# Weights cut to their own widths, shorter spreads, and a planner with other numbers, in a four-layer image kernel

## The chip, the cores and the metric

The kernel runs on one core of a Trainium2 chip. A core has TensorE (matrix products; PE in the profile, PEld for its weight loads), VectorE (DVE), ScalarE (ACT), GpSimd (POOL) and SyncE (SP, which issues transfers). The metric is the device time of one execution in microseconds (us); lower is better.

## The reference

The input is four images of 96 channels and 64x64 pixels. They go through four layers; the parts that this change touches are:

```python
# layer 0: normalize, 3x3 depthwise conv + SiLU, four-direction selective scan, gate, project
delta = softplus(dts + delta_bias)
def step(h, inp):                       # along 4096 pixels, for 192 channels x 16 states x 4 directions
    h = exp(d_t[..., None] * A) * h + (d_t * u_t)[..., None] * b_t[:, :, None, :]
    return h, einsum('bkdn,bkn->bkd', h, c_t)
...
# layer 1: deformable 3x3 convolution
v00, v01, v10, v11 = gather(y0, x0), gather(y0, x0 + 1), gather(y0 + 1, x0), gather(y0 + 1, x0 + 1)
sample = (1-wy)*(1-wx)*v00 + (1-wy)*wx*v01 + wy*(1-wx)*v10 + wy*wx*v11
...
# layer 2: Fourier mixing over the pixels, then a feed-forward layer in 8-bit floats
# layer 3: linear attention, then the same kind of feed-forward layer
```

Offsets and masks of layer 1 (27 values a pixel) come from a 3x3 convolution over 96 channels. Before most layers each pixel is normalized over its channels.

## The kernel before

The program is built by a planner in Python. One chain of units is the scan: 4 images x 4 directions x 4 stretches of 1024 pixels x 3 groups x 8 = 1536 units. Each unit spreads its inflow over 128 partitions with TensorE, multiplies and scans on VectorE, weighs on GpSimd, and is folded by TensorE:

```python
    def inflow(self, u):
        u.spread = self.net.clock.add(PE, 1.1, self.scanned[1])
        db = self.ps.tile([128, 2, CH], F32, name=f"db{u.key}", tag="db", bufs=2)
        for h in range(2):
            self.net.nc.tensor.matmul(db[:, h, :], lhsT=self.rep[:96, u.s % 4, :],
                rhs=u.du[u.s // 4][:, h * CH : (h + 1) * CH], start=True, stop=True)      # L872
    def recur(self, u):
        ...
        nc.vector.tensor_mul(u.db, u.db, u.bc[:, 0, :])                                   # L885
        nc.vector.tensor_tensor_scan(u.along(u.hh), u.along(u.da), u.along(u.db), first, ALU.mult, ALU.add)  # L888
    def weigh(self, u):
        ...
        self.net.nc.gpsimd.tensor_mul(u.hh, u.hh, u.bc[:, 1, :])                          # L897
    def total(self, u, v):
        ...                                    # 8 products of 32 columns into py, L915
```

The order in which a unit's parts are emitted[...]:

```python
            for stage, m in ((self.inflow, n + 1), (self.decay, n + 1)):
                if at(m) is not None:
                    stage(at(m))
            if n % 2 == 1 and at(n - 5) is not None:
                self.total(at(n - 5), at(n - 4))
```

Between the units two streams of side work are let in: one runs the work ahead of the scan and the layers 2 and 3 of finished images, the other the end of layer 0 and layer 1. A virtual clock decides how much, from costs written at each step (`cost(pe=2.4)`), from how far an engine may be ahead, and from a pace per unit:

```python
PE, DVE, ACT, POOL = range(4)
AHEAD = (2.0, 1.5, 3.0, 4.0)
BESIDE = 6.0
PACE = 4.9
...
    def has_room(self, work, ready):
        ...
        return all(not w or e <= now + a for w, e, a in zip(work, self.ends, AHEAD))
```

When the scan is over, the rest of the side work runs alone.

Many weights are padded with zero columns to 128[...], and the rows of the result that belong to the padding are not read:

```python
    def wide(m, n=128):
        return np.concatenate([m, np.zeros((*m.shape[:-1], n - m.shape[-1]))], axis=-1).astype(f)
    ...
    a["wom"] = wide(om.transpose(1, 2, 0))      # 27 columns of offsets and masks -> 128
    a["wdc"] = wide(...)                        # 96 -> 128
    a["cen96"] = wide(np.eye(96) - 1.0 / 96)
```

The normalization: centre with a product (L457), square, sum each chunk's squares into a row of its own with a mostly zero weight (L468), take the root, and spread the row back over the partitions (L483):

```python
            pc = self.mm(f"lnc{key}_{j}")
            nc.tensor.matmul(pc, lhsT=cen, rhs=x[:, cs], start=True, stop=True)            # L457
            ...
            nc.tensor.matmul(var, lhsT=self.to_row[C][:C, 7 - j : 135 - j], rhs=sq, ...)   # L468: 128 columns, one not zero
    ...
    def spread(self, rstd, j, n, key):
        pb = self.mm(f"lnb{key}_{j}")
        row = self.ident[:, j : j + 1].to_broadcast([128, 128])
        self.nc.tensor.matmul(pb, lhsT=row, rhs=rstd, start=True, stop=True)               # L483
        return pb[:n]
```

The offset convolution of layer 1, nine products a chunk, and the step sizes of layer 0, whose weight holds seven rows that are not zero among 103:

```python
                    nc.tensor.matmul(po, lhsT=wom[:, k, :],
                        rhs=pad[:, r0 + dy : r0 + dy + NR, dx : dx + W], ...)              # L1118
    ...
            nc.tensor.matmul(o, lhsT=dtw[:, k, m], rhs=xdbl[q, j], start=True, stop=True)  # L734
```

The sampling multiplies the gathered corners by their weights and sums the four by transposes that accumulate in one bank:

```python
                        for c in range(4):
                            nc.tensor.matmul(pt[:, k, :], lhsT=g[:, k0 + k, c * C : (c + 1) * C], rhs=net.ident,
                                is_transpose=True, start=(c == 0), stop=(c == 3))          # L1241
```

Of the kernel before, what the change touches and what calls it, by code (L numbers as in the profile page):

```python
# [20 lines left out]
L = H * W  # L21
# [23 lines left out]
def prepare(x, **w):  # L45
# [4 lines left out]
    def wide(m, n=128):  # L50

        return np.concatenate([m, np.zeros((*m.shape[:-1], n - m.shape[-1]))], axis=-1).astype(f)

# [27 lines left out]
    a["w_in"] = c(np.concatenate([wi[:, :128], wi[:, 128:192], wi[:, 128:192], wi[:, 192:], np.zeros((C, 64))], axis=1).astype(f))  # L81
# [3 lines left out]
    xpp = np.zeros((2, 128, DI), f)  # L85
# [3 lines left out]
    xpp[:, 64 + R + 1 : NX] = xp[2:, R:]  # L89
# [4 lines left out]

    dtp = np.zeros((NX, KG, DI), f)
    dtp[2 * NS : 2 * NS + R + 1, :2] = dtw[:2].transpose(2, 0, 1)
    dtp[64 : 64 + R + 1, 2:] = dtw[2:].transpose(2, 0, 1)
    a["dtw"] = dtp
# [7 lines left out]
    a["wo_a"] = wide(wo[:128])  # L106
    a["wo_c"] = wide(wo[128:])
# [4 lines left out]
    a["wom"] = wide(om.transpose(1, 2, 0))  # L112
    ob = w["L1_conv_offset_b"]
    put(V_OMB, np.concatenate([ob[0::2], ob[1::2], w["L1_conv_mask_b"]]))
    a["wdc"] = wide(w["L1_conv_weight"].reshape(C, C, 9).transpose(1, 2, 0))
# [8 lines left out]
    a["w2"] = wide(w["L2_attn_w2"].T.reshape(2, 96, C).transpose(1, 0, 2))  # L124
    for n in (2, 3):
        a[f"f{n}w1"] = c(w[f"L{n}_ffn_W1"].T)
        a[f"f{n}w2"] = wide(w[f"L{n}_ffn_W2"].T.reshape(3, 128, C).transpose(1, 0, 2))
# [3 lines left out]
    a["wff"] = wide(w["L3_attn_Wff"])  # L131
# [5 lines left out]
    a["cen96"] = wide(np.eye(96) - 1.0 / 96)  # L137
    cen = (np.eye(DI) - 1.0 / DI).astype(f)
    a["cen_a"] = wide(cen[:128], 256)
    a["cen_c"] = wide(cen[128:], 256)  # L140
# [55 lines left out]
AHEAD = (2.0, 1.5, 3.0, 4.0)  # L196
# [3 lines left out]
PACE = 4.9  # L200
# [132 lines left out]
class Net:  # L333
# [3 lines left out]
    def __init__(self, ctx, tc, ins):  # L337
# [5 lines left out]
        for name in ("vecs", "ident", "cen96", "grp3"):  # L343
            setattr(self, name, self.load(name, self.const))

        self.to_row = {}
        for n in (C, DI):
            t = self.to_row[n] = self.const.tile([128, 135], F32, name=f"to_row{n}")
            nc.vector.memset(t, 0.0)
            nc.vector.memset(t[:, 7:8], 1.0 / n)  # L350
# [96 lines left out]
    def centred(self, x, cen, dst, key, pool, bias=None):  # L447
# [3 lines left out]
        var = self.mm(f"lnv{key}")  # L451
        self.hold(1)

        def chain(j):
            cs = slice(j * CH, (j + 1) * CH)
            pc = self.mm(f"lnc{key}_{j}")
            nc.tensor.matmul(pc, lhsT=cen, rhs=x[:, cs], start=True, stop=True)  # L457
            pc = pc[:C]
# [5 lines left out]
            else:  # L464
                nc.scalar.activation(sq, pc, AF.Square, bias=bias)
                nc.scalar.activation(d, view(pc), AF.Identity, bias=bias)
            yield cost(pe=1.1, act=1.2)
            nc.tensor.matmul(  # L468
                var, lhsT=self.to_row[C][:C, 7 - j : 135 - j], rhs=sq, start=(j == 0), stop=(j == NCH - 1)
            )  # L470
            yield cost(pe=1.0)

        yield from pipe(self, (chain(j) for j in range(NCH)), 2)
        self.rstd = pool.tile([128, CH], F32, name=f"lns{key}", tag="lns", bufs=1)
        nw = pool.tile([128, CH], F32, name=f"lnw{key}", tag="lnw", bufs=1)
        yield from self.inv_sqrt_steps(self.rstd, var, nw, 128)
        self.hold(-1)

    def spread(self, rstd, j, n, key):

        pb = self.mm(f"lnb{key}_{j}")
        row = self.ident[:, j : j + 1].to_broadcast([128, 128])
        self.nc.tensor.matmul(pb, lhsT=row, rhs=rstd, start=True, stop=True)  # L483
        return pb[:n]
# [24 lines left out]
class Layer0:  # L509
# [48 lines left out]
    def before(self, b):  # L558
        net = self.net
        tc, nc, ins = net.tc, net.nc, net.ins  # L560
        with tc.tile_pool(name=f"l0u{b}", bufs=1) as up:
# [3 lines left out]
            with tc.tile_pool(name=f"l0b{b}", bufs=1) as sm:  # L565
                xp_a, xp_c = (net.load(q, sm) for q in ("xp_a", "xp_c"))
                dtw = net.load("dtw", sm)
# [33 lines left out]
    def normed_rows(self, b, x, pad, rows, as_rows):  # L601
# [3 lines left out]
        with tc.tile_pool(name=f"l0n{b}", bufs=2) as sm:  # L605
# [7 lines left out]
            cen = sm.tile([C, 128], F32, name=f"cen{b}", tag="cen", bufs=1)  # L613
# [3 lines left out]
            pb = net.mm(f"cb{b}")  # L617
            nc.tensor.matmul(pb[:, 0:1], lhsT=cen, rhs=mean, start=True, stop=True)
            bias = sm.tile([C, 1], F32, name=f"cenb{b}", tag="cenb", bufs=1)
            nc.scalar.mul(bias, pb[:C, 0:1], -1.0)  # L620
# [6 lines left out]
            def chain(j):  # L627
                pb = net.spread(rs, j, C, f"0_{b}")
                yield cost(pe=1.2, holds=1)
# [8 lines left out]
    def convolved(self, b, pad, xa, xc, rows, as_rows):  # L638
# [3 lines left out]
        with tc.tile_pool(name=f"l0i{b}", bufs=1) as sm:  # L642
            wc = sm.tile([C, 9, 256], F32, name=f"wc{b}", tag="wc")
            nc.sync.dma_start(wc, self.wc_d)
            wz = sm.tile([C, 256], F32, name=f"wz{b}", tag="wz")
# [4 lines left out]
            def chain(j):  # L650
                cs = slice(j * CH, (j + 1) * CH)
                r0 = j * NR
                for g in range(2):
                    pp = net.mm(f"pc{g}_{b}_{j}")
                    for q in range(9):
# [8 lines left out]
                        if q in (2, 5):  # L664
                            yield cost(pe=2.4, holds=1)
# [11 lines left out]
                    yield cost(pe=2.4, act=4.0, new=True, takes="zt" if g else "")  # L677
                zts = []
                for g, (c0, n) in enumerate(((0, 128), (128, D2))):
                    pz = net.mm(f"pz{g}_{b}_{j}")  # L680
                    nc.tensor.matmul(pz, lhsT=wz[:, c0 : c0 + 128], rhs=rows(pad, j), start=True, stop=True)
                    zt = sm.tile([128, CH], F32, name=f"zt{g}_{b}_{j}", tag=f"zt{g}")
                    nc.scalar.activation(zt[:n], pz[:n], AF.Silu)
                    zts.append((c0, n, zt))
                net.exp_and_log()
                yield cost(pe=2.0, act=3.8)
# [8 lines left out]
    def projected(self, b, j, us, xp_a, xp_c, sm, xdbl):  # L695
# [5 lines left out]
        for q in (1, 0):  # L701
# [3 lines left out]
            px = net.mm(f"px{b}_{q}_{j}")  # L705
            nc.tensor.matmul(px, lhsT=xp_a[:, q, :], rhs=ua, start=True, stop=False)
            nc.tensor.matmul(px, lhsT=xp_c[hp], rhs=us[2][hp, cs], start=False, stop=True)
            nc.scalar.activation(xd, px[:NX], AF.Identity, bias=net.vec(V_X1, NX))
            xdbl[q, j] = xd
            yield cost(pe=2.8, act=0.7, new=q == 1)  # L710
# [5 lines left out]
    def steps(self, b, ks, j, us, dtw, sm, xdbl):  # L716
# [14 lines left out]
        for k in ks:  # L731
            q = k % 2
            o, m = (pd[64 * q : 64 * q + 64], slice(128, DI)) if both else (pd, slice(0, 128))
            nc.tensor.matmul(o, lhsT=dtw[:, k, m], rhs=xdbl[q, j], start=True, stop=True)  # L734
# [7 lines left out]
        yield cost(pe=2.2 if both else 1.1, act=3.4, holds=1, takes="rl")  # L742
# [33 lines left out]
    def scan(self):  # L776
# [18 lines left out]
        for n in range(len(units) + 7):  # L795
# [6 lines left out]
            if n == 0:  # L802
# [4 lines left out]
                self.inflow(at(0))  # L807
            for stage, m in ((self.inflow, n + 1), (self.decay, n + 1)):
                if at(m) is not None:
                    stage(at(m))  # L810
            if n % 2 == 1 and at(n - 5) is not None:
                self.total(at(n - 5), at(n - 4))
# [55 lines left out]
    def inflow(self, u):  # L868
        u.spread = self.net.clock.add(PE, 1.1, self.scanned[1])
# [29 lines left out]
    def total(self, u, v):  # L899

        nc = self.net.nc
        self.net.clock.add(PE, 1.5 + 1.3 * (u.i == 0), max(u.weighed, v.weighed))
# [34 lines left out]
    def behind(self, b):  # L937
# [6 lines left out]
        with (  # L944
# [4 lines left out]
            for j0 in range(NCH - HB, -1, -HB):  # L949
# [15 lines left out]
                var = net.mm(f"va{b}_{j0}")  # L965
                key = f"o{b}_{j0}"

                def centred(i):
# [12 lines left out]
                    for g, (o, c0, n) in enumerate(((ca, 0, 128), (cc, 128, D2))):  # L981
                        pc = net.mm(f"pc{g}{b}_{j}")
                        ms = slice(c0, c0 + 128)
                        nc.tensor.matmul(pc, lhsT=cen_a[:, ms], rhs=ya, start=True, stop=False)
                        nc.tensor.matmul(pc, lhsT=cen_c[:, ms], rhs=yc, start=False, stop=True)
                        pc = pc[:n]
# [699 lines left out]
```

## Time and profile before

| | |
|---|---|
| time, median of 3 runs | 9619.79 us (9617.22 to 9630.14) |
| mean granted TensorE clock | 0.767 of full |
| scan, first to last unit | 356 to 8188 us, 1536 units |
| instructions | 92316 |
| moved from and to HBM | 1346.94 and 256.29 MB |

Costliest groups (line, engine, operation, result from operands, shape, count, then busy us and mean ns of one):

```profile
L897 POOL TENSOR_TENSOR hh<-hh,bc 128x1024 f32<-128x1024 f32 x1536 | 3667.4, 2389 | 341.8 <-DVE hh L888 229.2
L888 DVE TENSOR_TENSOR_SCAN hh<-da,st,db 128x1024 f32<-128x1024 f32 x1152 | 2703.7, 2347 | 365.0 <-ACT da L866 196.7
L872 PE MATMUL db<-du,rep 96*128 96x512 bf16 x3072 | 1172.9, 473 | 1531.8 <-DVE hh L888 1372.3
```

In a matmul's shape, 96*128 is the weight (rows used, columns) and 96x512 the moving operand. A float32 product appears as two MATMUL records. After the second bar stands the idle time of the engine just before the group and what ended most of it.

### The profile page before, as it was taken

What the parts mean: (1) busy time and instruction counts of PE and PEld (TensorE: products, weight loads), DVE (VectorE), ACT (ScalarE), POOL (GpSimd) and SP (SyncE); (2) the same over time, 40 slices, a digit from 0 to 9 for tenths busy, and PEclk for the clock granted to TensorE, in tenths of its full rate; (3) what the DMA queues carried; (4) which work ended last, traced back from release to release, by engine and by line L of the source; (5) the groups of instructions that cost most, each with busy time, mean ns of one, the idle gap of its engine ahead of it and who ended that gap; (6) DMA issues with size and microseconds to landing.
All of it is one profiled execution on the core that took longest, in us unless ns stands there. A gap on an engine that the chain in (4) does not pass through costs nothing.

```text
span 9618.0 us, 92316 instructions
## 1 busy us (share of the span) xinstructions
PE 6838.2 (71%) x31928; PEld 3124.9 (32%) x31928; DVE 7027.1 (73%) x4707; ACT 4082.4 (42%) x5574; POOL 6730.8 (70%) x4947
## 2 busy tenths in 40 slices
PE   6465855696756667867565787777767787788787
PEld 2111311131212233312122454323335542377474
DVE  0488778877888888778888887788878888332313
ACT  3563656465544333555433233453332345311323
POOL 0696589766889999678899995566989656376101
PEclk8555966696767678967666787877878887989887
DMA  1466676776777778777777787767777776354010
GB/s 48 139 188 168 172 189 193 184 185 177 207 195 191 204 200 206 189 183 205 195 199 203 195 212 172 182 159 190 192 189 198 192 184 168 86 145 130 16 54 11
DMA packets 775819, 1609.47 MB, mean 167 GB/s; under 512 B 247666, under 2 KB 338830, under 8 KB 773239
## 3 DMA queue, kind: packets, MB, share of 16 engines
q10 hardware_dynamic: 300672, 985.79, 40.5%
q1 hardware_dynamic: 400950, 391.20, 14.9%
q0 software_dynamic: 73728, 226.57, 8.8%
q8 instruction: 254, 4.16, 0.2%
q14 instruction: 215, 1.75, 0.1%
HBM read 1346.94 MB, written 256.29 MB: 167 GB/s over the span
## 4 chain that ended last, share of the span: by engine, by line
POOL 29%; PE 25%; DVE 16%; DMA 14%; issue 8%; ACT 5%; ACTq 1%; SPq 1%; DVEq 0%; POOLq 0%
POOL hh L897 13%; POOL g L1218 7%; DVE hh L888 7%; DMA da<-de 4%; DVE db L885 4%; PE pc L657 4%; PE ps L1241 3%; PE f L1332 3%; PE py L915 2%; PE db L872 2%; POOL lw L745 2%; DMA du<-du 2%; PE po L1118 2%; POOL st L895 1%; POOL w L744 1%
## 5 line engine op out<-in xcount | busy, mean ns | idle before, releaser
L897 POOL TENSOR_TENSOR hh<-hh,bc 128x1024 f32<-128x1024 f32 x1536 | 3667.4, 2389 | 341.8 <-DVE hh L888 229.2
L888 DVE TENSOR_TENSOR_SCAN hh<-da,st,db 128x1024 f32<-128x1024 f32 x1152 | 2703.7, 2347 | 365.0 <-ACT da L866 196.7
L872 PE MATMUL db<-du,rep 96*128 96x512 bf16 x3072 | 1172.9, 473 | 1531.8 <-DVE hh L888 1372.3
L866 ACT ACTIVATE da<-da,w_al 128x1024 f32<-128x1024 f32 x1536 | 1734.3, 1145 | 816.8 <-DMA da<-de 457.0
L885 DVE TENSOR_TENSOR db<-db,bc 128x1024 f32<-128x1024 f32 x1536 | 1866.9, 1215 | 278.0 <-PE db L872 275.9
L1218 POOL DMA_INDIRECT g<-table,idx x1152 | 1414.1, 1228 | 308.6 <-issue 226.8
L915 PE MATMUL py<-hh,w_fold 128*32 128x512 f32 x6144 | 1226.2, 809 | 121.6 <-POOL hh L897 98.8
L872 PEld LDWEIGHTS <-rep 96*128 96x128 bf16 x3072 | 275.4, 106 | 2633.9 <-issue 1521.2
L1241 PE MATMUL ps<-w_ident,g 128*96 128x128 f32 x4608 | 729.7, 325 | 342.8 <-DVE g L1227 180.7
L888 DVE TENSOR_TENSOR_SCAN hh<-da,db 128x1024 f32<-128x1024 f32 x384 | 878.1, 2287 | 125.4 <-ACT da L866 73.8
L1227 DVE TENSOR_TENSOR g<-g,wt 128x3456 f32<-128x3456 f32 x128 | 550.6, 4302 | 377.8 <-DMA g<-table,idx 361.4
L1241 PEld LDWEIGHTS ps<-w_ident,g 128*96 128x96 f32 x4608 | 639.6, 153 | 533.6 <-DVE g L1227 231.3
L895 POOL COPY st<-hh 128x1 f32<-128x1 f32 x1152 | 314.6, 273 | 642.6 <-DVE hh L888 619.1
L1249 ACT COPY st<-ps 96x384 f32<-96x384 f32 x384 | 182.1, 476 | 1182.8 <-PE ps L1241 1108.8
L657 PE MATMUL pc<-pad,wc 96*128 96x512 f32 x1152 | 544.0, 620 | 49.2 <-DMA wc<-wc_d 43.7
L1478 POOL CAST xqf<-fl 96x512 fp8e5<-96x512 f32 x64 | 51.2, 806 | 733.3 <-DVE fl L1436 635.5
L744 POOL TENSOR_TENSOR w<-w,ex 128x512 f32<-128x512 f32 x192 | 248.2, 1293 | 383.7 <-ACT w L741 383.2
L915 PEld LDWEIGHTS py<-hh,w_fold 128*32 128x32 f32 x6144 | 173.8, 126 | 719.6 <-issue 372.9
L768 DVE TENSOR_TENSOR du<-ex,du 128x512 bf16<-128x512 f32 x192 | 266.1, 1386 | 190.2 <-ACT du L766 186.6
L734 PE MATMUL pd<-xd,w_dtw 103*64 103x512 f32 (+1 forms) x512 | 316.3, 922 | 68.1 <-DMA w_dtw<-in_dtw 32.0
L747 DVE SCALAR_TENSOR_TENSOR rl<-pd,lw 128x512 f32<-128x512 f32 x192 | 130.0, 677 | 301.3 <-POOL lw L745 296.2
L657 PEld LDWEIGHTS pc<-pad,wc 96*128 96x128 f32 x1152 | 222.8, 198 | 344.6 <-issue 327.4
(241 smaller groups left out, 9366.1 us busy)
## 6 DMA issues: line engine op xcount, KB each, us to landing
da<-de ACTq DMA_DIRECT2D x1536, 512.0 KB
du<-du ACTq DMA_DIRECT2D x384, 192.0 KB
bc<-bcd ACTq DMA_DIRECT2D x128, 512.0 KB
du<-du SPq DMA_DIRECT2D x128, 384.0 KB
y<-yb SPq DMA_DIRECT2D x384, 128.0 KB
de<-rl SPq DMA_DIRECT2D x128, 256.0 KB
m<-in_dft SPq DMA_DIRECT2D x128, 256.0 KB
du<-du SPq DMA_DIRECT2D x128, 192.0 KB
```

Source lines behind the costliest of these rows:

```text
L657: nc.tensor.matmul(pp, lhsT=wc[:, q, g * 128 : (g + 1) * 128], rhs=pad[:, r0 + dy : r0 + dy + NR, dx : dx + W], start=(q == 0), stop=(q == 8),
L744: nc.gpsimd.tensor_sub(w1, w1, ex)
L866: self.net.nc.scalar.activation(u.da, u.da, AF.Exp, scale=self.al[:, a : a + 1])
L872: self.net.nc.tensor.matmul(db[:, h, :], lhsT=self.rep[:96, u.s % 4, :], rhs=u.du[u.s // 4][:, h * CH : (h + 1) * CH], start=True, stop=True,)
L885: nc.vector.tensor_mul(u.db, u.db, u.bc[:, 0, :])
L888: nc.vector.tensor_tensor_scan(u.along(u.hh), u.along(u.da), u.along(u.db), first, ALU.mult, ALU.add)
L895: self.net.nc.gpsimd.tensor_copy(u.state[:, u.n : u.n + 1], u.hh[:, last : last + 1])
L897: self.net.nc.gpsimd.tensor_mul(u.hh, u.hh, u.bc[:, 1, :])
L915: nc.tensor.matmul(py[p0 : p0 + 32], lhsT=self.fold[:, u.i, :], rhs=hc[:, h * CH : (h + 1) * CH], start=u.sums["add"] is None and u.i == 0 ...
L1218: nc.gpsimd.indirect_dma_start(out=g[:, k, :], out_offset=None, in_=self.tables[b % 2], in_offset=bass.IndirectOffsetOnAxis(ap=idx[:, 9 * ...
L1227: nc.vector.tensor_mul(g4, g4, w4.unsqueeze(2).to_broadcast([128, 36, C]))
L1241: nc.tensor.matmul(pt[:, k, :], lhsT=g[:, k0 + k, c * C : (c + 1) * C], rhs=net.ident, is_transpose=True, start=(c == 0), stop=(c == 3),)
```

## The change

The four corners of the sampling are summed by accumulating transposes in both kernels; that part of the code is the same. The change takes the padding out of the weights: each has its own number of columns, and result tiles have only the rows that are used. The variance rows are made by weights of 8 columns, the spread reads 8 rows, and the step sizes read only their 7 rows. It is meant to leave out work on zeros. With it go other numbers for the planner (costs, AHEAD, PACE), another order of fold and spread in a unit, and an own single buffer for one result. Cut to its core:

```diff
-    a["wom"] = wide(om.transpose(1, 2, 0))
+    a["wom"] = c(om.transpose(1, 2, 0))
... (so too wo_a, wo_c, wdc, w2, f2w2, f3w2, wff, cen96, cen_a, cen_c, w_in)
-    dtp = np.zeros((NX, KG, DI), f)
-    dtp[2 * NS : 2 * NS + R + 1, :2] = dtw[:2].transpose(2, 0, 1)
-    dtp[64 : 64 + R + 1, 2:] = dtw[2:].transpose(2, 0, 1)
-    a["dtw"] = dtp
+    a["dtw"] = c(dtw.transpose(2, 0, 1))
...
-AHEAD = (2.0, 1.5, 3.0, 4.0)
+AHEAD = (1.0, 1.5, 3.0, 2.0)
-PACE = 4.9
+PACE = 4.7
...
-                var, lhsT=self.to_row[C][:C, 7 - j : 135 - j], rhs=sq, ...
+                var, lhsT=self.selv96[:C, j, :], rhs=sq, ...
-        row = self.ident[:, j : j + 1].to_broadcast([128, 128])
+        row = self.ident[:k, j : j + 1].to_broadcast([k, n])        # k = 8
...
-                            yield cost(pe=2.4, holds=1)              # three products of the convolution
+                            yield cost(pe=1.5, holds=1)
... (so too most other cost(pe=...): 1.2 to 0.9, 2.7 to 1.4, 2.6 to 1.5, 1.1 to 0.8)
-            nc.tensor.matmul(o, lhsT=dtw[:, k, m], rhs=xdbl[q, j], start=True, stop=True)
+            rows = slice(64, 64 + R + 1) if h else slice(2 * NS, 2 * NS + R + 1)
+            nc.tensor.matmul(o, lhsT=dtw[rows, q, m], rhs=xdbl[q, j][rows], start=True, stop=True)
...
+            if n % 2 == 1 and at(n - 5) is not None:
+                self.total(at(n - 5), at(n - 4))
             for stage, m in ((self.inflow, n + 1), (self.decay, n + 1)):
                 if at(m) is not None:
                     stage(at(m))
-            if n % 2 == 1 and at(n - 5) is not None:
-                self.total(at(n - 5), at(n - 4))
...
-        u.spread = self.net.clock.add(PE, 1.1, self.scanned[1])
+        u.spread = self.net.clock.add(PE, 0.9, self.scanned[1])
-        self.net.clock.add(PE, 1.5 + 1.3 * (u.i == 0), max(u.weighed, v.weighed))
+        self.net.clock.add(PE, 1.6, max(u.weighed, v.weighed))
...
-                    nc.vector.tensor_add(xr, po[:C], xr)
+                    xo = op.tile([C, CH], F32, name=f"xo{b}_{j}", tag="xo", bufs=1)
+                    nc.vector.tensor_add(xo, po, xr)
```

## The prediction

> **What bounds the kernel now.** I read the engine lines and the slices first, then the time by stage, then who waits for whom.
>
> ```profile
> PE 6838.2 (71%) x31928; PEld 3124.9 (32%) x31928; DVE 7027.1 (73%) x4707; ACT 4082.4 (42%) x5574; POOL 6730.8 (70%) x4947
> ...
> PE   6465855696756667867565787777767787788787
> ...
> DVE  0488778877888888778888887788878888332313
> ...
> PEclk8555966696767678967666787877878887989887
> ```
>
> No engine is full over the whole span. VectorE stands at eight tenths while the scan runs (slices 2 to 34), then falls to three; TensorE stands at seven or eight to the end. PEclk is the granted TensorE clock in tenths: it moves between 5 and 9. The next view sums busy time by stretch; the columns are length, then PE, PEld, DVE, ACT, POOL, and last clock, DMA share and GB/s.
>
> ```profile
> 2295.00:4273.00 1978.00, 1347.03 (x4986) 515.27 (x4985) 1666.14 (x1026) 891.02 (x1136) 1667.27 (x1221) 0.74 0.76 197
> 6254.00:8188.00 1934.00, 1445.10 (x7584) 704.53 (x7582) 1637.88 (x1032) 761.69 (x1055) 1456.48 (x1054) 0.80 0.73 183
> 8188.00:8860.00 672.00, 537.92 (x3609) 403.74 (x3608) 221.94 (x204) 147.44 (x292) 407.69 (x327) 0.88 0.44 121
> 9120.00:9618.00 498.00, 404.85 (x3032) 286.06 (x3030) 135.73 (x192) 139.60 (x272) 45.60 (x35) 0.82 0.12 36
> ```
>
> The first two are the scans of images 1 and 3: VectorE is busy 84%, so a scan of 384 units takes about 1980 us where its VectorE work alone is 1666. From 8188 us on there is no scan: 1430 us in which TensorE is busy 81% and VectorE 31%. **The scan is VectorE's with some waits in it; the tail is TensorE's.** In the scan VectorE's waits are these:
>
> ```profile
> DVE hh L888 <- ACT da L866: 266.0, 141, 13.2
> DVE db L885 <- PE db L872: 265.6, 131, 28.2
> DVE du L768 <- ACT du L766: 165.2, 82, 6.9
> ```
>
> 265.6 us of the scan is VectorE waiting for TensorE's `db` spread, which stands in TensorE's queue behind side work. So a slower TensorE is already felt there.
>
> **What sets TensorE's speed.** The clock records are only ever 0.5 or 1.0, in pieces of 3.41 us. Lines of `db` and of the offset convolution show what each costs (min/median/max ns):
>
> ```profile
> L872 PE MATMUL db<-du,rep x3072: 375/388/635, 349.6 to 8183.1; 96*128 96x512 bf16 x192
> ...
> L1118 PE MATMUL po<-pad,w_wom x576: 589/592/1223, 2534.7 to 8344.6; 96*128 96x512 f32 x192
> ```
>
> I sorted the instructions by the record they fall in: a float32 512-column piece has median 592 ns at 1.0 and 1061 at 0.5, and back-to-back starts are 429 and 854 ns apart. Now the same view by stretch, twice with a like busy share:
>
> ```profile
> 400.00:800.00 400.00, 218.06 (x562) 46.46 (x563) 327.83 (x222) 234.91 (x329) 362.91 (x280) 0.58 0.67 183
> 7000.00:7200.00 200.00, 117.24 (x556) 60.89 (x557) 152.87 (x87) 67.46 (x95) 173.31 (x119) 0.76 0.72 188
> 8273.00:8345.00 72.00, 72.00 (x220) 33.79 (x220) 11.74 (x20) 16.95 (x36) 7.91 (x8) 1.00 0.39 75
> ```
>
> TensorE is busy 55% and 59% in the first two, yet the clock is 0.58 and 0.76. The first stretch is mostly 32-column `py` pieces; the second has sampling transposes and Fourier products. So I fitted the record of each 3.41 us window to the columns streamed in the window before, one coefficient per shape (rows*columns). They come out near the filled share of the array: 128*128 29.7, 96*128 23.8, 64*128 12.0, 103*64 11.2, 128*32 8.1. **Activity is streamed columns times filled area**, and a threshold of 0.36 of a full array at full clock tells 95% of the windows. At 0.5 a full array gives at most 0.5, a 96*128 weight 0.375, just enough to get the clock back; a 96*27 weight gives 0.08 at 0.5 and 0.16 at 1.0, never enough. (96 columns are unsure: 25.4 with an error of 3 for 128*96.)
>
> [...]here the 128*96 transposes have coefficient 32.0, as a full array[...]. [...]here 128 columns load in 198 ns (L657), 96 in 153 (L1241), 32 in 126 (L915). [...]
>
> **The change, part by part.** The corner sums are the same in both: accumulating transposes. What differs:
>
> 1. **Weights lose their padding.** 128 columns become 96 (L457, L1029/1030, L1255, L1417, L1500, L1563), 8 (the variance rows L468, L991), 27 (the offset convolution L1118), and the spread L483 has 8 rows in place of 128. The steps' L734 has 7 rows in place of 103. Streaming takes as long as before, since moving columns are unchanged; the weight load shrinks where it isn't hidden, about 0.1 us for each of some 450 variance and spread products that stand alone: 45 us of TensorE time at most, perhaps 20 on the path.
> 2. **The clock falls.** I went through the trace's matmuls in order, each from its recorded start or the end of the one before, and worked out each window's activity with the new areas and from it the next window's clock by the threshold (0.32 to keep a clock of 1.0). Unchanged kernel: clock 0.778 (measured 0.767), streaming 5669 us. Changed, with 96 columns counted as 128: 0.726 and 6147 us, +478. With 96 counted as 96: 0.694 and 6477, +808. Largest: L1118 264 to 406, L483 202 to 280, L872 901 to 963 or 992, L915 936 to 994 or 1023, L468 150 to 180 or 216. The last ones before it are not changed themselves; they run in windows that lost their clock.
>    By stage: the tail goes from 879 to 1036 or 1142 (+157 to +263), the scan from 4791 to 5111 or 5335 (+320 to +544).
>    On the path: in the tail TensorE is 81% busy and the chunks of one layer form a chain, so I take 0.8: +125 to +210. In the scan side work has slack while VectorE works, but `db` stands behind it; I take 0.4: +130 to +220. Sum +255 to +430, middle +340.
> 3. **The planner's numbers.** TensorE costs go down (three convolution products 2.4 to 1.5 us, where six records of 429 ns make 2.57 even at full clock), AHEAD for TensorE 2.0 to 1.0 and for GpSimd 4.0 to 2.0, PACE 4.9 to 4.7. The cheaper costs and the smaller lead roughly cancel. PACE is below what the scan takes (7832 us by 1536 units is 5.10), so fewer side steps per unit would at best win some of 0.2 x 1536 = 307 us in the scan and give most back in the tail. I take -60 with a wide error.
> 4. **The fold before the spread.** `total` now precedes `inflow`: TensorE may stand still for GpSimd (98.8 us of waits for `hh` before) ahead of the next `db`. I take +20 for it and the single `xo` buffer.
>
> 9620 + 340 - 20 - 60 + 20 = 9900.
>
> **Rivals.** (a) *The clock hardly matters*: VectorE and GpSimd set the scan, TensorE's 30% idle takes up the loss, only the tail pays. For it: VectorE at 84% in the scan. Against it: its 265.6 us of waits for `db`. Then 9620 + 125 - 80 = 9665. (b) *The clock latches low*: 96 columns count as 96, so 96*96 work at 0.5 reaches 0.28 and never gets back; lateness also lowers activity further. Then +808 of streaming with half of it on the path and a fuller planner: 10100 to 10200. (c) *The smaller pace wins*: the scan shortens to 4.9 us a unit, 300 us less, and the tail doesn't grow: 9600. Against it: image 1's last layers end at 8367 us, after the scan, so the other chain of work is already late. (d) *Unused columns and shorter loads slow TensorE for nothing*: then the new kernel is 20 to 60 us faster. Against it: pieces of 512 columns start 429 ns apart with loads of 198 ns under them.
>
> **Range and chances.** The main line and (b) are both slower by more than 2% (over 9812); (a) and (c) are within 2%; only (c) with (d) would be faster by 2%. I give main and (b) together 0.72, (a) and most of (c) 0.25, and 0.03 to faster. The range runs from (a) to between (b)'s ends: 9660 to 10180.
>
> **What would show it.** Right: mean clock 0.69 to 0.73 in place of 0.767; L1118's mean near 1060 in place of 640; L872 and L915 means up by 5 to 10% without any change of theirs; the tail 125 us longer or more; VectorE's wait for `db` up from 265.6. Wrong: a clock that stays at 0.76, or a fallen clock with a scan of the same length, or a scan under 5.0 us a unit. If GpSimd's waits end before TensorE's in the scan, the order of fold and spread was the larger part.

## The result, and the profile after

The changed kernel takes 9671.61 us (median of 4 runs), the kernel before 9620.47 beside it: ratio 1.0055, 95% interval 1.0037 to 1.0072. It is slower by half a per cent, where 2.9% was predicted. The measured time lies just inside the stated range, near its lower end; the predicted loss of 280 us was five and a half times the measured 51.

The same lines of the page as before: engine totals, TensorE's busy slices, VectorE's, and the granted clock.

```profile
PE 7101.8 (73%) x31928; PEld 2904.9 (30%) x31928; DVE 6993.7 (72%) x4673; ACT 4105.5 (42%) x5606; POOL 6733.5 (70%) x4947
...
PE   7565966696766568776767778778777777887798
...
DVE  0488688867788887888788888777888888523313
...
PEclk9556855686667678765778788778888777897796
```

TensorE is busy 264 us longer with as many instructions; the mean clock is 0.749 in place of 0.767. Now the busy time by stretch, first of the changed kernel and then of the kernel before, each split at the end of the scan (columns as in the prediction; last are clock, DMA share and GB/s).

```profile
357.00:8354.00 7997.00, 5793.83 (x24550) 2123.96 (x24552) 6578.94 (x4186) 3622.45 (x4768) 6209.40 (x4524) 0.73 0.73 186
8354.00:9671.50 1317.50, 1077.33 (x6960) 701.98 (x6954) 378.29 (x430) 326.80 (x646) 472.94 (x376) 0.81 0.27 74
```

```profile
356.00:8190.00 7834.00, 5473.04 (x23568) 2221.27 (x23568) 6546.17 (x4129) 3542.32 (x4624) 6188.00 (x4507) 0.75 0.73 189
8190.00:9618.00 1428.00, 1157.79 (x7938) 821.55 (x7938) 444.25 (x519) 384.05 (x758) 491.60 (x393) 0.86 0.26 74
```

The scan became 163 us longer and **the tail 110 us shorter**, against the prediction. The counts in brackets say why: some 980 matmuls moved out of the tail (7938 to 6960) into the scan (23568 to 24550). Next are TensorE groups of the changed kernel.

```profile
L869 PE MATMUL db<-du,rep 96*128 96x512 bf16 x3072 | 1204.1, 486 | 1222.3 <-DVE hh L885 1091.4 <-DMA du<-du 100.5 <-DMA da<-de 10.2
...
L1115 PE MATMUL po<-pad,w_wom 96*27 96x512 f32 x576 | 274.3, 625 | 4.5 <-DVE d L1378 2.4 <-ACT pix L1133 2.1
...
L476 PE MATMUL lnb<-lns,w_ident 8*96 8x512 f32 x192 | 156.5, 954 | 25.5 <-DVE lns L403 24.3 <-DVE tl L1433 1.2
```

L1115 is the offset convolution, now with 27 columns. The prediction had it near 1060 ns; it takes 625 (640 before), so it runs mostly at full clock: in stretches at a clock of 1.00 its records take 593 ns, and 597 with 128 columns in the kernel before. L476 is the spread, now with 8 rows: 954 ns in place of 716. Last, VectorE's largest wait in the scan:

```profile
DVE db L882 <- PE db L869: 526.4, 224, 17.2
```

That wait doubled, from 265.6 us in the scan of the kernel before.

So there are two questions: what the clock follows, if not the columns, and what made scan and tail change places. Theory A is the prediction's (rows times columns), theory R says that only rows count; beside them stand the planner's numbers, the order and the buffer.

### The profile page after: what moved, and what is told of

Same layout as the page of the kernel before. It is cut to its first block, busy times and chain, and to the rows that moved or that the text cites. A ratio compares the mean times of both kernels' runs of the same rounds, so it can differ in the third digit from the quotient of the medians.

```text
span 9671.5 us, 91970 instructions
## 1 busy us (share of the span) xinstructions
PE 7101.8 (73%) x31928; PEld 2904.9 (30%) x31928; DVE 6993.7 (72%) x4673; ACT 4105.5 (42%) x5606; POOL 6733.5 (70%) x4947
## 4 chain that ended last, share of the span: by engine, by line
PE 30%; POOL 21%; DVE 18%; DMA 16%; issue 8%; ACT 5%; ACTq 1%; SPq 1%; DVEq 0%; POOLq 0%
POOL hh L894 10%; DVE hh L885 7%; POOL g L1215 6%; DVE db L882 4%; PE pc L653 4%; PE ps L1238 4%; DMA da<-de 3%; DMA du<-du 3%; PE f L1329 2%; PE po L1115 2%; PE py L912 2%; PE db L869 2%; DMA g<-table,idx 2%; DVE g L1224 2%; POOL lw L742 1%
## 5 line engine op out<-in xcount | busy, mean ns | idle before, releaser
L869 PE MATMUL db<-du,rep 96*128 96x512 bf16 x3072 | 1204.1, 486 | 1222.3 <-DVE hh L885 1091.4
L1215 POOL DMA_INDIRECT g<-table,idx x1152 | 1444.9, 1254 | 431.5 <-issue 227.8
L912 PE MATMUL py<-hh,w_fold 128*32 128x512 f32 x6144 | 1292.7, 807 | 263.5 <-POOL hh L894 144.3
L869 PEld LDWEIGHTS <-rep 96*128 96x128 bf16 x3072 | 207.5, 104 | 2674.1 <-DVE hh L885 1841.5
L892 POOL COPY st<-hh 128x1 f32<-128x1 f32 x1152 | 288.1, 250 | 681.7 <-DVE hh L885 642.2
L731 PE MATMUL pd<-xd,dtw 7*64 7x512 f32 (+1 forms) x512 | 334.9, 968 | 45.4 <-DVE rl L744 41.0
L761 POOL TENSOR_TENSOR ex<-ex,du 128x512 f32<-128x512 f32 x192 | 224.7, 1170 | 141.2 <-ACT du L759 134.2
```

The source lines that it names most:

```text
L731: nc.tensor.matmul(o, lhsT=dtw[rows, q, m], rhs=xdbl[q, j][rows], start=True, stop=True)
L892: self.net.nc.gpsimd.tensor_copy(u.state[:, u.n : u.n + 1], u.hh[:, last : last + 1])
L912: nc.tensor.matmul(py[p0 : p0 + 32], lhsT=self.fold[:, u.i, :], rhs=hc[:, h * CH : (h + 1) * CH], start=u.sums["add"] is None and u.i == 0 ...
L1215: nc.gpsimd.indirect_dma_start(out=g[:, k, :], out_offset=None, in_=self.tables[b % 2], in_offset=bass.IndirectOffsetOnAxis(ap=idx[:, 9 * ...
```

## What the clock follows

**Matmuls alone, clock up.** A kernel with nothing but products of 512 columns:

```diff
+    for n in range(32):
+        for q in range(tiles):
+            nc.tensor.matmul(ps[c0 : c0 + cols], lhsT=w[:rows, c0 : c0 + cols], rhs=r[:rows], start=True, stop=True)
```

> Matmuls alone (the rest of the computation is left out): 32 products of 512 columns for each weight shape, once after a pause and one product (clock down), once after 20 full products (clock up). Theory A, as in the prediction: the clock follows streamed columns times rows times columns of the weight. Then 128*8, 128*32 on one column tile, 96*27 and 8*128 all fall to 0.5 after a window or two, records near 1060 ns, and 96*96 can't come up from 0.5. Theory R: only the rows count, for as long as they stream. Then 128*8, 128*32, 96*27 and 96*96 keep 1.0 (records near 592 ns) and come up from 0.5 within one to three windows, while 8*128, 8*96 and 32*128 fall to 0.5, and 64*128 keeps 1.0 when warm but stays at 0.5 when cold (0.25 of a full array at half clock, below the fitted threshold of 0.36).

The groups (count, two records for each product, then busy us and mean ns of one record; the weight stands as rows*columns):

```profile
L69 PE MATMUL qe<-re,w 8*128 8x512 f32 x128 | 105.3, 1018 | 0.0
L69 PE MATMUL qk<-rk,w 8*96 8x512 f32 x128 | 104.1, 1006 | 0.0
L69 PE MATMUL qd<-rd,w 32*128 32x512 f32 x128 | 100.3, 976 | 0.0
...
L69 PE MATMUL qh<-rh,w 128*32 128x512 f32 x128 | 55.3, 593 | 0.0
L69 PE MATMUL qj<-rj,w 96*27 96x512 f32 x128 | 55.3, 592 | 0.0
L69 PE MATMUL qi<-ri,w 128*8 128x512 f32 x128 | 55.3, 592 | 0.0
```

A weight of 128*8 streams as fast as one of 128*128 (592 ns for both), one of 8*128 at little more than half the speed (1018). Theory A is out for a clock that is up. The pauses of this run did not come about: nothing tied the next operand to them, and the profile shows 0.0 us of idle time before these groups and before the full products ahead of them. So the start from 0.5 stayed open.

**The same with true pauses, and more row counts.**

```diff
-            nc.scalar.copy(r, src)
+            nc.vector.scalar_tensor_tensor(r, pause, 0.0, src, ALU.mult, ALU.add)   # waits for the pause
```

> Matmuls alone again (the rest of the computation is left out), now with a real pause of some 12 us before each stretch, since in the first such run the pauses didn't come about and the cold half stayed untested. Weights of 128, 112, 96, 80, 64, 48 and 32 rows with 128 columns, and 96*27, 128*8, four tiles of 128*32, two of 64*64; each once from 0.5 and once after 20 full products. Theory R with the fitted threshold (0.36 of a full array to come up, 0.32 to stay): at 0.5 a weight of n rows gives n/256, so 128 and 112 and perhaps 96 rows come up (0.375), 80 and 64 rows stay at 0.5; at 1.0 it gives n/128, so 48 rows (0.375) and more stay at 1.0 and 32 rows (0.25) fall. 96*27 and 128*8 do as 96*128 and 128*128. If small columns count after all, those two stay at 0.5 from a cold start.

Stretches in this order: 96*128, 80*128 from 0.5; 64*128, 48*128 after full products, which are in the stretch and start at 0.5 themselves; 96*27, 128*8 from 0.5; last, two tiles of 64*64 at once from 0.5. The third number from the end is the mean clock.

```profile
247.00:278.50 31.50, 31.25 (x66) 13.45 (x66) 0.02 (x1) 0.14 (x1) 0.00 (x0) 0.91 0.00 1
359.50:416.50 57.00, 56.69 (x66) 22.07 (x66) 0.08 (x1) 0.14 (x1) 0.00 (x0) 0.50 0.00 0
570.80:619.00 48.20, 47.99 (x104) 20.49 (x104) 0.02 (x1) 0.10 (x1) 0.00 (x0) 0.94 0.00 0
709.70:779.00 69.30, 69.19 (x104) 27.64 (x104) 0.06 (x1) 0.00 (x0) 0.00 (x0) 0.65 0.00 0
956.30:988.00 31.70, 31.68 (x66) 7.47 (x66) 0.00 (x0) 0.00 (x0) 0.00 (x0) 0.90 0.00 1
1069.50:1101.00 31.50, 31.36 (x66) 6.37 (x66) 0.00 (x1) 0.04 (x1) 0.00 (x0) 0.91 0.00 1
1297.10:1352.00 54.90, 54.89 (x129) 14.78 (x128) 0.00 (x0) 0.00 (x0) 0.00 (x0) 0.50 0.00 0
```

96 rows come up after some 6 us (an estimate: a mean of 0.91 over 31.5 us is 5.7 us at 0.5), 80 don't in 57 us (0.50). With the clock up, 64 rows keep it (mean 0.94), and 48 lose it (0.65); there the fitted 0.32 was wrong, since 48 rows give 0.375. 96*27 and 128*8 come up like 96*128 (0.90 and 0.91). Two tiles of 64*64 that stream at the same time stay at 0.50 for 55 us; if the two were added up they would be 128 rows, more than the 96 that come up. So here they count once.

The kernels' own traces bear this out. For an estimate, take each float32 record of 512 columns to stream for 429 ns at full clock and 854 at half, the distance of back-to-back starts in the kernel before (256 columns: 216 and 427; 512 columns of 8-bit floats: 216 and 426; other lengths in proportion, bf16 as 8-bit floats), at most until the next one starts, and give each of the two rules the thresholds that suit it best. In the changed kernel, rows times streaming time in one piece of 3.41 us of the clock's record tell the clock of the next in 98% of the pieces at half clock and in 99.7% at full; the filled area, with tiles that stream together added up, tells 92% and 89%. In the kernel before the same figures are 97% and 98.5% for the rows, 94% and 98.3% for the area: there the two rules are hard to tell apart.

**In the kernel, columns only** (columns cut everywhere but in the variance rows; spread and steps left with their rows):

```diff
-    a["wom"] = wide(om.transpose(1, 2, 0))
+    a["wom"] = c(om.transpose(1, 2, 0))          # so too the other padded weights
```

> The kernel before with only the columns cut (27, 96, 103, 64 in place of 128; variance, spread and steps keep their 128 columns and their 128 or 103 rows), planner and order as before. Theory A: clock 0.70 to 0.74, time 1.5 to 4% longer, the offset convolution's records near 1000 ns. Theory R: clock 0.76 to 0.775, offset convolution near 640 ns, time within 0.3% of before.

Ratio 1.0018 (1.0007 to 1.0030), clock 0.765, the 27-column convolution 639 ns. Theory R holds, theory A, which had 1.5% at least, fails. What the 0.18% comes of was not followed up.

**In the kernel, rows only:**

```diff
-        row = self.ident[:, j : j + 1].to_broadcast([128, 128])
-        self.nc.tensor.matmul(pb, lhsT=row, rhs=rstd, start=True, stop=True)
+        row = self.ident[:8, j : j + 1].to_broadcast([8, 128])
+        self.nc.tensor.matmul(pb, lhsT=row, rhs=rstd[:8], start=True, stop=True)
...
-            nc.tensor.matmul(o, lhsT=dtw[:, k, m], rhs=xdbl[q, j], start=True, stop=True)
+            nc.tensor.matmul(o, lhsT=dtw[rows, q, m], rhs=xdbl[q, j][rows], start=True, stop=True)
```

> The kernel before with only the rows cut: the spread reads 8 rows in place of 128, the steps 7 in place of 103; columns, planner and order as before. Theory R: this is where the clock went, so 0.74 to 0.755 against 0.767, spread records near 950 ns in place of 730, and time 0.3 to 1% longer. Theory A: a part of the fall only, clock about 0.755, 0.3 to 0.8% longer. If the planner's numbers are what cost, the time stays within 0.2%.

Ratio 1.0056 (1.0037 to 1.0076), clock 0.741. The profiled execution, split at the end of the scan:

```profile
350.00:8189.00 7839.00, 5626.63 (x23568) 2216.80 (x23568) 6556.24 (x4129) 3541.22 (x4623) 6188.61 (x4507) 0.73 0.73 189
8189.00:9711.00 1522.00, 1257.05 (x7938) 863.66 (x7938) 444.98 (x519) 383.04 (x758) 487.09 (x393) 0.80 0.24 69
```

The schedule is that of before (the counts are equal), so this reads cleanly. In the scan TensorE is busy 154 us longer and the scan is 5 us longer; in the tail TensorE is busy 99 us longer and the tail is 94 us longer. **Here a slower TensorE costs almost nothing beside the scan (5 us for 154) and nearly all of itself after it (94 for 99).** (These are single executions, this one of 9711 us where the median of its runs is 9696. The kernel before alone ranged from 9586 to 9678 us, so the 5 and the 94 are good to some tens of us. Two more pairs below give the same picture.)

**The changed kernel with its rows undone:**

```diff
-        self.rstd = pool.tile([NCH, CH], F32, name=f"lns{key}", tag="lns", bufs=1)      # 8 rows to spread
+        self.rstd = pool.tile([128, CH], F32, name=f"lns{key}", tag="lns", bufs=1)
-                var, lhsT=self.selv96[:C, j, :], rhs=sq, ...
+                var, lhsT=self.to_row[C][:C, 7 - j : 135 - j], rhs=sq, ...
-            nc.tensor.matmul(o, lhsT=dtw[rows, q, m], rhs=xdbl[q, j][rows], start=True, stop=True)
+            nc.tensor.matmul(o, lhsT=dtw[:, k, m], rhs=xdbl[q, j], start=True, stop=True)
```

> The changed kernel with only its rows undone: the spread reads 128 rows, the variance rows have 128 columns so that there are 128 to read, the steps read 103. Columns, planner, order and buffer stay changed. Theory R: the rows cost at least what they cost in the kernel before (0.56%), so this is 0.5 to 1.3% faster than the changed kernel, ratio to before 0.992 to 1.000, clock back to 0.765 or more. If what the parts leave over (their sum is -0.23%, the whole +0.55%) is rows meeting the changed planner, it is all here: ratio 0.990 to 0.994.

Ratio 0.9970 (0.9959 to 0.9981), clock 0.777.

```profile
361.00:8340.00 7979.00, 5565.66 (x24544) 2163.42 (x24543) 6602.00 (x4186) 3623.56 (x4768) 6211.43 (x4524) 0.77 0.72 186
8340.00:9600.00 1260.00, 1005.53 (x6964) 706.55 (x6963) 378.97 (x431) 325.82 (x647) 471.70 (x376) 0.85 0.27 78
```

The counts are those of the changed kernel (24550 and 6960). With the rows cut, TensorE is busy 228 us longer in the scan, which is 18 us longer, and 72 us longer in the tail, which is 57 us longer. The rows cost the changed kernel 1.0055 - 0.9970 = 0.85%, more than its whole loss. Without them it beats the kernel before.

## What moved the work between scan and tail

**The planner's numbers alone** (costs, AHEAD, PACE):

```diff
-AHEAD = (2.0, 1.5, 3.0, 4.0)
+AHEAD = (1.0, 1.5, 3.0, 2.0)
-PACE = 4.9
+PACE = 4.7
-                            yield cost(pe=2.4, holds=1)
+                            yield cost(pe=1.5, holds=1)             # and the others
```

> The kernel before with only the planner's numbers of the changed kernel (TensorE costs, AHEAD, PACE); shapes and order as before. In the changed kernel the scan is 163 us longer and the tail 111 us shorter. Theory P: the numbers let more side work in beside the scan, so scan near 5.15 to 5.2 us a unit, tail near 1320 us, clock unchanged at 0.765 to 0.775, total within 0.5% either way. Rival: the longer scan comes of the lower clock alone, then scan and tail stay within 40 us of 7832 and 1430.

Ratio 0.9949 (0.9927 to 0.9972): a gain.

```profile
358.00:8369.00 8011.00, 5589.70 (x25146) 2312.93 (x25148) 6602.51 (x4196) 3633.51 (x4790) 6205.60 (x4525) 0.75 0.72 186
8369.00:9582.00 1213.00, 951.03 (x6360) 691.02 (x6360) 369.02 (x421) 313.04 (x623) 470.32 (x376) 0.85 0.28 79
```

With TensorE held for cheap, 1578 more matmuls go beside the scan (25146 against 23568). The scan grows by 177 us and the tail shrinks by 215. This is the exchange seen in the changed kernel.

**The same with the pace of before:**

```diff
-PACE = 4.7
+PACE = 4.9
```

> The kernel before with the changed kernel's TensorE costs and AHEAD, but the pace of before (4.9). If the gain of the planner's numbers comes from the pace, this is within 0.15% of before. If it comes from the costs and AHEAD, which let more side work in, ratio 0.994 to 0.997 with the scan even longer (5.25 us a unit or more) and the tail shorter than 1213 us.

Ratio 1.0113 (1.0086 to 1.0140), scan 8241 us (5.365 a unit), tail 1150. The scan grew further, as expected of costs and AHEAD, but the expected gain did not come: against pace 4.7 the scan lost 230 us and the tail gave back 63. So the smaller pace belongs to the cheaper costs.

**The pace alone,** on the kernel before:

```diff
-PACE = 4.9
+PACE = 4.7
```

> The kernel before with nothing changed but the pace, 4.9 to 4.7. With the changed kernel's costs and AHEAD the same step of the pace was worth 1.6% (ratio 1.0113 to 0.9949). Theory S (the time is scan plus the side work left over, and every one of the planner's numbers only moves the border): scan shorter than 7834 us by 50 to 150, tail longer than 1428 by about as much, time within 0.7% either way. Rival (pace as such gains): ratio 0.985 to 0.992 at an unchanged tail.

Ratio 1.0171 (1.0141 to 1.0202), more than either theory had.

```profile
356.00:7988.00 7632.00, 5223.90 (x20893) 1990.80 (x20892) 6469.63 (x4054) 3437.87 (x4409) 6168.22 (x4490) 0.74 0.75 192
7988.00:9784.00 1796.00, 1455.38 (x10612) 1052.90 (x10612) 522.30 (x627) 478.77 (x941) 513.86 (x410) 0.86 0.23 66
```

The scan is 202 us shorter, the tail 368 longer. Here side work put off costs more than it saves: in the tail TensorE is busy 81% of the time and VectorE 29%. A third point of the planner's curve, pace 4.6 with the changed costs:

```diff
-PACE = 4.7
+PACE = 4.6
```

> The kernel before with the changed kernel's planner numbers, but a pace of 4.6. Theory S: scan shorter than 8011 us, tail longer than 1213, ratio 0.990 to 1.003.

Ratio 1.0134 (1.0107 to 1.0160): scan 7922, tail 1473, the same exchange, and a larger loss than expected. So 4.6, 4.7, 4.9 give 1.0134, 0.9949, 1.0113: of these three 4.7 is by far the best.

**The order alone:**

```diff
+            if n % 2 == 1 and at(n - 5) is not None:
+                self.total(at(n - 5), at(n - 4))
             for stage, m in ((self.inflow, n + 1), (self.decay, n + 1)):
```

> The kernel before with only the fold put ahead of the spread in a unit. What the three parts measured so far leave over of the change (columns +0.18%, rows +0.56%, planner -0.51%, together +0.23, the whole +0.55) is +0.3%. Theory O: the order makes it: VectorE's wait for the db spread rises from 267 us to 350 or more, scan 20 to 60 us longer, time +0.2 to +0.6%. Rival: the parts don't add up, the order alone stays within 0.15%.

Ratio 0.9954 (0.9937 to 0.9971): also a gain. VectorE's wait for `db` does rise, and the scan is 56 us longer:

```profile
DVE db L885 <- PE db L872: 452.3, 191, 25.3
```

But the tail is 65 us shorter and the clock 0.783. Why the clock rises with the order was not tried. The reverse in the changed kernel:

```diff
-            if n % 2 == 1 and at(n - 5) is not None:
-                self.total(at(n - 5), at(n - 4))
             for stage, m in ((self.inflow, n + 1), (self.decay, n + 1)):
                 ...
+            if n % 2 == 1 and at(n - 5) is not None:
+                self.total(at(n - 5), at(n - 4))
```

> The changed kernel with the order of before (spread, then fold). Theory O: 0.2 to 0.6% faster than the changed kernel, so within 0.3% of before (ratio 0.997 to 1.003), VectorE's wait for the db spread near 420 us in place of 526. Rival (no part of the order): ratio 1.005 as the changed kernel.

Ratio 1.0092 (1.0068 to 1.0115), slower than the changed kernel; the wait for `db` fell from 526.4 to 439.1 us, and the time rose all the same. Theory O is wrong in its sign: that wait does not tell what the order is worth.

**The buffer,** taken out of the changed kernel together with the planner's rule that only one chunk at a time may hold it (`takes="xo"`); on the kernel before it was not tried alone:

```diff
-                    nc.vector.tensor_add(xo, po, xr)
+                    nc.vector.tensor_add(xr, po, xr)
...
-                yield from pipe(self.net, (gated(i) for i in range(HB)), 2, xo=1)
+                yield from pipe(self.net, (gated(i) for i in range(HB)), 2)
```

> The changed kernel with the result of layer 0's last product written over the residual again, in place of its own single buffer. Theory X (the buffer holds the end of layer 0 back): 0.3 to 0.7% faster than the changed kernel, ratio 0.998 to 1.002. Rival (the buffer matters nothing): ratio within 0.15% of 1.0055.

Ratio 1.0161 (1.0126 to 1.0196). The buffer with its rule gains 1.06%; both theories are wrong. Without it the tail is 1404 us in place of 1317, the scan 8029 in place of 7997, and 7544 matmuls are left for the tail in place of 6960. Whether the memory or the planner's rule makes this was not parted.

**Pairs.** Planner and rows:

```diff
+AHEAD = (1.0, 1.5, 3.0, 2.0)
+PACE = 4.7                                              # and the changed kernel's costs
+        row = self.ident[:8, j : j + 1].to_broadcast([8, 128])      # and steps of 7 rows
```

> The kernel before with the planner's numbers and the cut rows together; columns, order and buffer as before. If the two add up: ratio 0.9949 x 1.0056 = 1.0005. If the rows cost more under the planner that holds TensorE for cheap: 1.005 to 1.012, with the scan at 5.25 us a unit or more.

Ratio 0.9986 (0.9973 to 0.9998): nearly the sum. Beside the planner alone, TensorE is busy 178 us longer in a scan of 8004 us (8011 before), and 43 us longer in a tail that is 34 us longer (1247). Planner and order on the padded weights:

```diff
+AHEAD = (1.0, 1.5, 3.0, 2.0)
+PACE = 4.7                                              # and the changed kernel's costs
+            if n % 2 == 1 and at(n - 5) is not None:    # ahead of inflow and decay
+                self.total(at(n - 5), at(n - 4))
```

> The kernel before, weights padded as they are, with the changed kernel's planner numbers and order: the two parts that gained alone (0.9949 and 0.9954). If they add up 0.990; if both win the same shorter tail, 0.992 to 0.995. Clock 0.775 or more. It should beat both kernels.

Ratio 1.0052 (1.0026 to 1.0079): the two gains together lose. Is that the border again? The pair at two other paces:

```diff
-PACE = 4.7
+PACE = 4.6          # and 4.8 in the run after it
```

> Planner numbers and order of the changed kernel on the padded weights, as in the run that gave 1.0052, with a pace of 4.6. If the loss of that pair is a mechanism of the order under cheap TensorE costs, the ratio stays at 1.003 or more. If it is where the border between scan and tail happened to fall, one step of the pace moves it by 0.5% or more either way.

> Planner numbers and order of the changed kernel on the padded weights, now with a pace of 4.8 (4.7 gave 1.0052, 4.6 gave 1.0075). Theory S: the order has moved the best pace up, so 4.8 leaves less for the tail: tail at or under 1260 us and ratio 0.993 to 1.001. If the pair loses by a mechanism of its own, the ratio stays at 1.003 or more here too.

1.0075 (1.0051 to 1.0099) and 1.0046 (1.0034 to 1.0057). The pair loses at each of the three paces, so by the expectation it isn't the pace's border alone. At 4.8 the tail is 1165 us, shorter than expected, but the scan takes 8112. The changed kernel with its rows undone, by the same steps:

> The changed kernel with its rows undone (ratio 0.997) and a pace of 4.6. Theory S: within 0.7% of 0.997 either way, with scan and tail moving against each other.

> The changed kernel with its rows undone and a pace of 4.8 (4.7 gave 0.997, 4.6 gave 1.0093). Theory S: near its best, ratio 0.993 to 1.003, scan longer than 7979 us and tail shorter than 1260.

1.0093 (1.0062 to 1.0125) and 1.0034 (1.0019 to 1.0050) around 0.9970; the swing at 4.6 is larger than expected. Scan and tail are 7940 and 1387 us at 4.6, 7979 and 1260 at 4.7, 8111 and 1173 at 4.8.

These runs tell more about the pair. At 4.7 it leaves 7540 matmuls for the tail, as many as the changed kernel without its buffer (7544); with buffer and cut columns, which is the kernel with its rows undone, 6964 are left, and the ratio is 0.9970. At 4.6 and 4.8 the pair and that kernel leave nearly the same (7984 and 7970; 5220 and 5236), and their times agree within the noise. **By the counts, what the pair lacks at 4.7 is the buffer.** The pair with the buffer alone was not run, and why the buffer moves the border there and not at 4.6 or 4.8 stays open. The runs at pace 4.7 can be put in a row from one kernel to the other:

| | ratio | scan, us | tail, us | matmuls left for the tail |
|---|---|---|---|---|
| before (pace 4.9) | 1 | 7834 | 1428 | 7938 |
| + planner's numbers | 0.9949 | 8011 | 1213 | 6360 |
| + order | 1.0052 | 8007 | 1319 | 7540 |
| + columns and buffer | 0.9970 | 7979 | 1260 | 6964 |
| + rows: the changed kernel | 1.0055 | 7997 | 1317 | 6960 |

In another sequence the same steps have other sizes. The changed kernel with the order of before leaves 6360 matmuls for the tail, as the planner's numbers alone do, and yet it takes 1.4% longer (1.0092 against 0.9949), of which the rows explain 0.4% (0.9986). The rest is not explained.

The fastest versions measured are the kernel before with the planner's numbers (0.9949) or with the order (0.9954); their intervals overlap.

## Why the prediction was wrong, step by step

- **The weights lose their padding; the clock falls (parts 1 and 2).** The step that failed is "activity is streamed columns times filled area". In the runs rows counted and columns didn't (clock 0.741 with the rows cut, 0.765 with the columns, 0.767 before). The trace of before hardly tells these apart: most of its float32 weights of 32 or 64 columns stream in groups of four or two at once (those of `py` at L915 start within 30 ns of each other in 1314 groups of four and 428 of two, those of 103*64 at L734 in 127 groups of two), and I counted each as a stream of its own. Four times the coefficient of 128*32 (8.1) is 32, and twice that of 103*64 (11.2) is 22: those of 128 and 103 full rows. I read "a quarter of the columns" where "a quarter of the time" stood. One coefficient did speak against the area, and I passed over it: 128*96 transposes had 32.0, as a full array, where three quarters of 29.7 would be 22. So L1118, L468 and the 96-column weights were wrongly in the sum; the clock fell to 0.749, not to 0.69 to 0.73. That the spread and the steps would lower the clock was right, since there rows were cut: with the rows alone it is 0.741. The weight loads did get shorter (204 to 109 ns at the offset convolution, 210 to 92 at the variance rows), but of the -20 for them nothing shows: with the columns alone the kernel is 0.18% slower, some 17 us.
- **On the path: 0.4 in the scan, 0.8 in the tail.** The rows-only run gives 5 of 154 us (0.03) and 94 of 99 us (0.95); the changed kernel against its rows undone 18 of 228 (0.08) and 57 of 72 (0.79). So the share in the tail was about right and the share in the scan wrong, and TensorE's own time grew by less than the +320 to +544 and +157 to +263 of the prediction. The terms "+130 to +220" and "+125 to +210" measured 5 and 94 in the rows-only execution; of the +340 in the sum, the rows cost some 82 us in the changed kernel (0.85%). The 265.6 us of waits for `db` were no proof that TensorE's speed is felt: with rows cut and the clock lower they were 285.1. This was rival (a), which I gave too little. Its 9665 us, so near the measured 9671.61, is luck all the same: it had the tail 125 us longer, and it became 110 us shorter while the scan grew by 163.
- **The planner's numbers: -60 with a wide error.** Measured -0.51%, some -49 us: right in size, but by chance. I expected a shorter scan given back in the tail; what came was a longer scan and a shorter tail, because the lower costs and the smaller lead, which I said cancel, together lengthen the scan by 407 us at the pace of before (8241), and the pace takes back only 230 of it.
- **The fold before the spread and the buffer: +20.** Wrong in sign for the order alone (-0.46%) and for the buffer inside the changed kernel (-1.06%). The order has no one worth: on top of the planner's numbers, without the buffer, it costs 1.0%.
- **The signs named beforehand.** L1118 (now L1115) near 1060 ns: no (625). L872 and L915 up by 5 to 10%: 473 to 486 (2.7%) and 809 to 807 ns, no. Mean clock 0.69 to 0.73: no, 0.749. The tail longer by 125: no, shorter by 110. VectorE's wait for `db` up: yes, but it rose with the planner alone (392.7) and the order alone (452.3), and by only 20 us with the lower clock alone (285.1).

The +0.55% is thus rows (+0.85% where they are undone in the changed kernel) against the rest of the change, which without them gains 0.30%: in the sequence of the table, planner and order together lose 0.52%, and buffer and columns win 0.82%. The single parts do not add up to that gain; planner, order and buffer each change how much is left for the tail.

## What to carry to other kernels

Before a coefficient fitted to a trace is carried over to another shape, ask which two causes always came together in that trace; one small kernel that parts them is worth more than the fit. In these runs padding a weight's columns bought no clock (0.765 without it, 0.767 with it); rows were what to keep up (0.767 with them, 0.741 without), and that was worth 94 of 99 us of TensorE's time after the scan and 5 of 154 beside it. A planner's cost, lead and pace belong together: here 0.1 of pace alone moved the time by up to 1.9% (0.9949 to 1.0134), more than the whole change did.

## What the runs showed of the hardware

In these runs the granted clock followed the rows of the weights and the time in which they streamed: from 0.5, 96 rows brought 1.0 back after some 6 us of unbroken products (an estimate from a mean clock of 0.91 over 31.5 us) and 80 rows did not in 57 us (0.50); at 1.0, 64 rows kept it and 48 lost it (mean clock 0.94 and 0.65 with the full products ahead of them). Columns had no part in it down to 8 (128*8: 592 ns a record with the clock up, mean clock 0.91 from 0.5), and two column tiles of 64*64 that streamed side by side counted once (0.50 over 55 us). A float32 record of 512 columns took 592 ns at full clock and 1061 at half (medians in the changed kernel).
